# A graph network with nucleus attention on one core: a fifth row buffer, and step 2 turns its rows by VectorE and DRAM

## The chip, the cores and the metric

The kernel runs on one core of a Trainium2 chip. The core has TensorE (PE, with its weight loads shown as PEld), VectorE (DVE), ScalarE (ACT), GpSimd (POOL) and SyncE (SP, which here issues nearly all DMAs). The metric is the device time of one execution in microseconds; lower is better. All data are float32.

## The reference

There are N = 3327 nodes with 256 features. Two layers follow one another, each with a layer norm and a ReLU ahead of it and a residual around it. Layer 0 makes two steps; each multiplies one state by a row-normed copy of the adjacency (R) and another by a top-p attention matrix (A), which is made new in each step.

```python
def _top_p_attention(X, W1, W2, W3):
    logits = (X @ W1.T @ W2.T) @ (X @ W3.T).T
    probs = softmax(logits)
    # keep the largest of each row until they hold 0.9 of its sum
    ...
    return A / A.sum(-1)

R = S + eye; R = R / R.sum(-1)
Z = 0; Xf = X; Xa = X
for n in range(2):
    A = _top_p_attention(Xa, W1, W2, W3)
    Xf = R @ Xf
    Xa = A @ Xa
    Z = Z + Xf @ U1[n].T + Xa @ U2[n].T
h = layernorm(X + Z) * ln_g + ln_b
```

Layer 1 is attention over the neighbours of the adjacency with four heads (leaky ReLU, softmax over neighbours, ELU).

## The kernel before

The 3327 rows are padded to 26 tiles ("rows" below) of 128. The program has three stages. **Step 1** and **step 2** (`n` = 0 and 1) are the two steps of layer 0. The **last stage** is layer 1: four blocks of 832 target nodes, each a loop over 26 source tiles, with masks on ScalarE, exponents on VectorE (L1733) and products on PE (L1749, L1763).

A row of a step goes through this chain:

- `Row.logits` (PE, L898) multiplies the row's queries with all keys into PSUM. The operands are `qq` (queries of all rows) and `kt` (keys), both held twice, on the two halves of the partitions. `exps` (ACT, L913) writes the exponentials into a buffer `e`, 128 x 3328. There are four such buffers.
- A threshold for the top-p cut is searched: `count` (ACT, L950) counts above a threshold, `step` (L952 to L996) makes the next threshold from the count with short instructions on one column. The first two thresholds of a row are stepped on GpSimd; step 2 has a third, stepped on VectorE. Starting values come from `stats` (L809), which gets mean and variance of each row's logits from the keys' moments `gk`.
- `window`, `sort` and `choose` (VectorE, L1006 to L1059) find the exact cut in the values under the threshold. `drop` (VectorE, L1064) zeroes what is cut off, in four parts.
- The row must be turned[...]. `BLOCKED` (L50) says in how many rows of each step this is done by blocks; before the change it is (26, 0). With blocks, `turn_blocks` (VectorE, L1102) turns 32x32 blocks in place, `put_blocks` writes 1024 columns to DRAM (L1106), and four `get_blocks` (L1111) read them back rearranged; `attend_blocks` (PE, L1118) multiplies. Only the last two column tiles go through PE. Without blocks, `turn` (PE, L1077) turns 128x128 pieces by the identity into PSUM, ACT or DVE copies them to `et` (L1088), and `attend` (PE, L1095) multiplies.
- In step 1, `finish1` makes keys and queries of step 2 from the result, and the values `ys` (first half: the next step's right operand, fetched later as `rhs`; second half: the part of Z). In step 2, `finish2` adds up, norms and projects for layer 1.

Beside it, `full` computes R @ Xf for each row: loads of the transposed adjacency (`at`, four buffers), 26 matmuls into `accf` (L1142), and an evacuation: ACT copies `accf` to `f` (L1149) or DVE adds to it straight from PSUM (L1154). `add` then completes it on DVE: in step 1 the division by the row sum (L1169 to L1171, into `c`), in step 2 a multiply and add with a `base` fetched from `ys` (L1173, into `main`). `project_u` has multiplied `main` and `c` by the U1 matrices beforehand, so step 2's full products go straight into Z.

The order of all instructions is found by a planner (`Plan`, L472). Each piece of work is `put` with an engine, a length, a rank, what it needs, and the buffers it takes and gives back; `lag` is the reckoned time from its end until its result can be used. `either` lets the planner choose ACT or DVE. The planner runs these through a clock and writes the queues in that order; on the chip each engine then takes its instructions in that fixed order. Full products have the rank min(1 + 1.15 t, 27) in step 1, and rows the rank of their number (step 2: plus 30), lower first.

Of the kernel before, what the change touches and what calls it, by code (L numbers as in the profile page):

```python
# [15 lines left out]
ALU = mybir.AluOpType  # L16
# [33 lines left out]
BLOCKED = (NT, 0)  # L50
# [537 lines left out]
def fast(  # L588
# [31 lines left out]
    kts = spill.tile([P, NT * P], F32, name="kts")  # L620
    qqs = spill.tile([P, NT, P], F32, name="qqs")
# [26 lines left out]
    with ExitStack() as l0:  # L648
# [17 lines left out]
        qq = wpool.tile([P, NT, P], F32, name="qq")  # L666

# [5 lines left out]
        u2 = wpool.tile([P, 2, 2 * D], F32, name="u2")  # L673
# [3 lines left out]
        gk = wpool.tile([P, 2 * DA + 1], F32, name="gk")  # L677
        GP.memset(gk, 0.0)
        GP.tensor_copy(gk[:DA, DA + 1 :], ident[:DA, :DA])
# [22 lines left out]
        def weights():  # L702
# [10 lines left out]
            for n in range(STEPS):  # L713
                cols = slice((1 - n) * D, (2 - n) * D)
                uloads.append(
                    plan.put(
                        "SP", 0.4, -196.5 + n, nc.sync.dma_start, u1[:, :, cols],
                        u1t[n].rearrange("(c p) o -> p c o", p=P), lag=8.0,
                    )
                )  # L720
                plan.put(
                    "SP", 0.4, -150.0, nc.sync.dma_start, u2[:, :, cols], u2t[n].rearrange("(c p) o -> p c o", p=P)
                )
# [25 lines left out]

        def layer1_loads():  # L750
# [24 lines left out]
        def moments(t, kq, ps_k, ps_g):  # L775
# [4 lines left out]
            held = {}  # L780
# [28 lines left out]
        def stats(lo, hi, rank, needs, scaled):  # L809
# [6 lines left out]
            def product(held, t0, m):  # L816

                held["ps"] = ps_x.tile([P, 3, 2 * DA + 1], F32, name="px")
                for k in range(m):
                    T.matmul(held["ps"][:, k, :], qq[:, t0 + k, :], gk, start=True, stop=True)  # L820
# [6 lines left out]
            def square(held, t0, m):  # L827
                qg = held["qg"]
                for k in range(m):
                    junk = small.tile([P, DA], F32, name="qj", bufs=1)  # L830
                    V.scalar_tensor_tensor(
                        junk, qg[:, k, :DA], 1.0, qg[:, k, DA + 1 :], ALU.mult, ALU.mult,
# [4 lines left out]
            for t0 in range(lo, hi, 3):  # L837
                held, m = {}, min(3, hi - t0)
# [24 lines left out]
            return plan.put("DVE", 0.6, rank, rest, needs=[a])  # L863

        plan = Plan(dict(rows=1, mvs=3, pl=2, px=2, acca=1, accf=1, et=3, at=4, y=1, e2=3, mask=2, **BUFS))

        class Row:
# [10 lines left out]
            def open(self):  # L878
                self.e = epool.tile([P, NP], F32, name="e")
# [6 lines left out]
            def logits(self, k):  # L886
# [7 lines left out]
                for r in range(2):  # L894
# [5 lines left out]
                        qq[half, self.i, :],  # L900
# [51 lines left out]
            def step(self, k, eng):  # L952
# [16 lines left out]
                else:  # L969
                    TS(self.q, t, (self.t0, self.t1)[k - 1], 0.5, ALU.add, ALU.mult)  # L970
                    TS(self.u, s[k], s[k - 1], self.q, ALU.subtract, ALU.mult)
# [8 lines left out]
                else:  # L980
# [5 lines left out]
                TS(self.q, self.g, 0.5, 1.0 / AIM[self.n], ALU.mult, ALU.add)  # L986
                invert(self.q)
# [136 lines left out]
        JC = 4  # L1124

        class Full:
# [24 lines left out]

            def take(self):
                self.f = small.tile([P, H * FH + 2 * H], F32, name="f", bufs=BUFS["f"])
                V.tensor_add(self.f[:, :D], self.acc[:, :D], self.src[:, self.t, :D])  # L1154
                if self.n == 0:
                    V.tensor_copy(self.f[:, D : D + 1], self.acc[:, D:])
# [6 lines left out]
            def add(self):  # L1163
# [4 lines left out]
                if self.n == 0:  # L1168
                    V.tensor_scalar(rs, self.f[:, D : D + 1], 1.0, None, ALU.add)  # L1169
                    V.reciprocal(rs, rs)  # L1170
                    V.scalar_tensor_tensor(here, f, rs, here, ALU.mult, ALU.add)  # L1171
                else:
                    V.scalar_tensor_tensor(main[:, self.t, :D], f, rs, self.base, ALU.mult, ALU.add)  # L1173
# [4 lines left out]
        def keys_summed(t, kq, ps_k, ps_g, rank, needs, tags, give):  # L1178
            turn, copy, product, gather = moments(t, kq, ps_k, ps_g)
# [32 lines left out]
        def prepare(t, measured):  # L1212
# [28 lines left out]
            def keys():  # L1241
                GP.tensor_copy(kt[mine, cols], held["kq"][mine])
                GP.tensor_copy(qq[other, t, :], held["kq"][other])

            def double():
                nc.sync.dma_start(qq[mine, t, :], held["kq"][other])
# [7 lines left out]
            k = plan.put("POOL", 0.7, r, keys, needs=[a])  # L1254
            q = plan.put("SP", 0.2, r, double, needs=[a])
            g = t % 4 == 0 and keys_summed(
                t, lambda: held["kq"], lambda: ps_a.tile([P, P], F32, name="acca"),
# [3 lines left out]
            return [k, q], g  # L1261
# [18 lines left out]
        def finish1(row, done, rank):  # L1280
# [27 lines left out]
            def queries():  # L1308
                GP.tensor_copy(qq[other, t, :], held["kq"][other])

            def spread():
                kq = held["kq"]
                if not direct:
                    nc.sync.dma_start(kts[mine, cols], kq[mine])
                    nc.sync.dma_start(qqs[other, t, :], kq[other])
                nc.sync.dma_start((qq if direct else qqs)[mine, t, :], kq[other])

            def project_u2():
                ps = held["pu"] = ps_x.tile([P, 2 * D], F32, name="px")
                for k in range(2):  # L1320
                    T.matmul(ps, held["xt"][:, k, :], u2[:, k, :], start=(k == 0), stop=(k == 1))
# [5 lines left out]
            def add():  # L1327
                y = held["y"]
                GP.tensor_add(y[:, 1, :], y[:, 1, :], rhs[0][:, t, :])

# [14 lines left out]
            kq = [a]  # L1345
            if direct:
                kq = [
                    plan.put("DVE", 0.2, r, keys, needs=[a, drawn[0]]),
                    plan.put("POOL", 0.4, r, queries, needs=[a, drawn[0]]),
                ]  # L1350
            kq.append(plan.put("SP", 0.3, r, spread, needs=[a, drawn[0] if direct else None]))
            g = t % 4 == 0 and keys_summed(
                t, lambda: held["kq"], lambda: ps_x.tile([P, P], F32, name="px"),
                lambda: ps_x.tile([P, DA + 1], F32, name="px"), r, [a, guessed[0]], ("px", "px"), [],
            ) or None
            plan.put("SP", 0.02, r, lambda: None, needs=[kq, g], give=["kq"], lag=0.0)
            a = plan.put("PE", 1.75, r + 0.1, project_u2, needs=[x_], take=["px"])
            a = plan.put("ACT", 0.56, r + 0.1, stage, needs=[a], take=["ystage"], give=["px", "xt"])
            a = plan.put("POOL", 0.8, r + 0.3, add, needs=[a])
            y = plan.put("SP", 0.1, r + 0.3, store, needs=[a], give=["ystage"], lag=3.0)  # L1360
            return kq, g, y

        def fetch_keys(r):
            half = slice(r * DA, r * DA + DA)
            w = max(half_of(t)[2].stop for t in range(LAST + 1) if side(t) == r)
            nc.sync.dma_start(kt[half, :w], kts[half, :w])

        def fetch_queries(lo, hi):
            nc.sync.dma_start(qq[:, lo:hi, :], qqs[:, lo:hi, :])
# [6 lines left out]
        def finish2(row, done, z, rank):  # L1376
# [64 lines left out]
            x_ = plan.put("SP", 0.1, r - 1.5, fetch, needs=[row.pieces["guess"]], take=["ystage"], lag=3.0)  # L1441
# [4 lines left out]
            s_ = plan.put("SP", 0.1, r, store, needs=[a])  # L1446
# [35 lines left out]
        def search(row, rank, keys, stats_of, fresh):  # L1482
# [4 lines left out]
            for g in range(2):  # L1487

                def logits(g=g):
# [4 lines left out]
                    "PE", 1.95 - 0.67 * g, rank - 2.5, logits, needs=[keys, fresh, a], take=["pl", "pl"] + ["e", "sc"] * (1 - g)  # L1494
# [10 lines left out]
            for j in range(2):  # L1505
# [4 lines left out]
                a = plan.put("POOL", (3.8, 4.7)[j], rank - (2.0, 1.6)[j], row.step, j, GP, needs=[got, more])  # L1510
# [21 lines left out]
        GROUPS = -(-NT // 4)  # L1532

        def attention(row, rank, total, drops, right):
            a = None
            if row.i < BLOCKED[row.n]:
                come = []
                for g in range(3):
                    b = plan.put("DVE", 1.25, rank - 1.001, row.turn_blocks, g, needs=[drops[g]])
                    b = plan.put("SP", 0.5, rank - 1.0, row.put_blocks, g, needs=[b], lag=3.5)  # L1540
                    b = plan.put("POOL", 0.02, -90.0, lambda: None, needs=[b], lag=0.0)
                    come.append(
                        [plan.put("SP", 0.45, rank - 1.0, row.get_blocks, g, o, needs=[b], lag=3.5) for o in range(4)]
# [6 lines left out]
                for j in (0, 4, 8, 12, 24, 16, 20):  # L1550
                    if j == 24:
# [4 lines left out]
                        take=["acca"] * (j == 0), give=["e"] * (j == 20),  # L1556
                    )
                return plan.put("ACT", 0.4, rank - 2.7, row.attended, needs=[a, total], take=["xa"], give=["acca", "sc"])
            for g in range(GROUPS):
# [4 lines left out]
                    give=["e"] * (g == GROUPS - 1),  # L1564
# [518 lines left out]
```

## Time and profile before

| what | us |
|---|---|
| three runs, median (lowest to highest) | 2159.17 (2158.55 to 2160.39) |
| the profiled execution | 2158.39 |
| its span | 2156.6 |
| first and last result of a row, step 1 (L1122) | 132.3 and 828.8 |
| first and last result of a row, step 2 (L1122) | 935.6 and 1674.4 |
| last matmul stage (L1749), main part from | 1676.9 |

The result of a row is its instruction at L1122, the only one per row that scales the attended sum. Between 828.8 and about 914 no row's attention runs: the keys of step 2 depend on all rows of step 1, and PE fills the time with full products. The mean granted TensorE clock is 0.995 of full speed. In the profile, a fp32 matmul appears as two instructions and a transpose as one. Instructions of PE overlap, so the mean ns of one is longer than its share of the queue; starts are the better measure.

### The profile page before, as it was taken

To read this page: it belongs to the slowest core of one execution; us is meant where nothing else is said; L and a number is where in the kernel's file an instruction comes from. 1 tells how busy PE (TensorE), PEld (TensorE's weight loads), DVE (VectorE), ACT (ScalarE), POOL (GpSimd) and SP (SyncE) were. 2 spreads that over 40 slices of the span, in tenths; PEclk is the share of its full clock that TensorE was granted. 3 is DMA by queue.
4 is the path that set the end of the run, shared out by engine and by line. 5 is a ranking of instruction groups with operands and counts; after the bars stand their busy time and mean duration, and the time that the engine had idled before them with its cause. 6 is when DMAs were issued, how large, how long until landed. Compare 5 with 4: busy or idle time off the path is not lost. (4 is left out here: it accounts for less than half of the span.)

```text
span 2156.6 us, 35324 instructions
## 1 busy us (share of the span) xinstructions
PE 2098.1 (97%) x11247; PEld 1464.1 (68%) x11247; DVE 1757.0 (81%) x4436; ACT 1324.9 (61%) x2444; POOL 945.9 (44%) x2259
## 2 busy tenths in 40 slices
PE   8999999999999999999999999999999999999997
PEld 6577777777777777778877888888888433333332
DVE  5579887878777781578999899978878999989895
ACT  4677565665456621687777767777773556565552
POOL 5367555555554630367667666567553100000001
PEclk9999999999999999999999999999999999999999
DMA  4077777777776796522222222222224545354441
GB/s 122 22 172 186 184 181 177 177 177 173 187 173 162 154 240 181 150 62 76 65 64 59 62 62 62 74 76 75 68 70 134 153 128 160 114 153 117 117 124 33
DMA packets 398243, 265.52 MB, mean 123 GB/s; under 512 B 181370, under 2 KB 352096, under 8 KB 398048
## 3 DMA queue, kind: packets, MB, share of 16 engines
q1 hardware_dynamic: 397152, 262.97, 47.1%
q8 instruction: 91, 1.49, 0.3%
q14 instruction: 104, 0.85, 0.1%
q10 hardware_dynamic: 896, 0.21, 0.0%
HBM read 205.31 MB, written 56.84 MB: 122 GB/s over the span
## 5 line engine op out<-in xcount | busy, mean ns | idle before, releaser
L950 ACT ACTIVATE junk<-e,sc 128x3327 fp8e5<-128x3327 f32 x182 | 558.2, 3067 | 65.2 <-POOL sc L995 64.0
L1095 PE MATMUL acca<-rhs,et 128*128 128x256 f32 x1456 | 336.4, 379 | 0.0
L1142 PE MATMUL accf<-main,at 128*128 128x257 f32 x1352 | 314.0, 383 | 8.3 <-DMA at<-in_adjt_dram 6.6
L1142 PE MATMUL accf<-c,at 128*128 128x256 f32 x1352 | 313.4, 382 | 3.5 <-DVE f L1154 2.5
L1118 PE MATMUL acca<-rhs,e 128*128 128x256 f32 x1248 | 284.6, 383 | 22.3 <-DMA e<-blocks 21.5
L1095 PEld LDWEIGHTS acca<-rhs,et 128*128 128x128 f32 x1456 | 268.9, 190 | 32.3
L1142 PEld LDWEIGHTS accf<-main,at 128*128 128x128 f32 x1352 | 252.0, 190 | 57.0 <-issue 10.9
L1142 PEld LDWEIGHTS accf<-c,at 128*128 128x128 f32 x1352 | 249.8, 190 | 49.1 <-issue 9.7
L1118 PEld LDWEIGHTS acca<-rhs,e 128*128 128x128 f32 x1248 | 243.8, 197 | 57.5 <-issue 23.6
L1006 DVE SCALAR_TENSOR_TENSOR y<-e,sc 128x1639 f32<-128x1639 f32 x104 | 208.6, 2006 | 58.2 <-POOL sc L992 55.9
L1011 DVE MAX8 cands<-y 128x8 f32<-128x205 f32 (+1 forms) x832 | 243.0, 362 | 3.6
L913 ACT ACTIVATE e<-pl 128x1024 f32<-128x1024 f32 x208 | 183.7, 889 | 68.4 <-PE pl L898 66.2
L1064 DVE SCALAR_TENSOR_TENSOR e<-e,thr 128x1024 f32<-128x1024 f32 x208 | 219.0, 1075 | 4.8 <-DVE thr L1059 2.8
L1888 POOL TENSOR_TENSOR qq<-qq 128x256 f32<-128x256 f32 x4 | 3.0, 756 | 446.3 <-ACT qq L1884 446.2
L1722 ACT ACTIVATE et<-at 128x448 bf16<-128x448 f32 (+1 forms) x204 | 112.2, 550 | 130.1 <-DVE e L1733 75.1
L1749 PE MATMUL pl<-e,main 128*64 128x416 f32 x1024 | 188.8, 516 | 0.0
L898 PE MATMUL pl<-kt,qq 64*128 64x512 f32 (+1 forms) x832 | 173.6, 535 | 0.0
L1749 PEld LDWEIGHTS pl<-e,main 128*64 128x64 f32 x1024 | 70.0, 137 | 109.4 <-issue 92.3
L1733 DVE SCALAR_TENSOR_TENSOR e<-c,low,et 128x832 f32<-128x832 f32 x128 | 128.9, 1072 | 6.3 <-issue 3.2
L898 PEld LDWEIGHTS pl<-kt,qq 64*128 64x128 f32 x832 | 71.5, 186 | 83.8 <-issue 75.7
L1721 ACT ACTIVATE at<-at 128x448 f32<-128x448 f32 (+1 forms) x204 | 110.5, 542 | 26.2 <-DMA at<-in_adjt_dram 26.2
L1088 ACT COPY et<-px 128x512 f32<-128x512 f32 (+1 forms) x129 | 67.3, 533 | 95.1 <-PE px L1077 47.8
(546 smaller groups left out, 3408.8 us busy)
## 6 DMA issues: line engine op xcount, KB each, us to landing
at<-in_adjt_dram SPq DMA_DIRECT2D x414, 256.0 KB
blocks<-e SPq DMA_DIRECT2D x78, 512.0 KB
e<-blocks SPq DMA_DIRECT2D x312, 128.0 KB
at<-in_adjt_dram SPq DMA_DIRECT2D x102, 192.0 KB
at<-in_adjt_dram SPq DMA_DIRECT2D x52, 128.0 KB
ys<-ystage SPq DMA_DIRECT2D x26, 256.0 KB
rhs<-in_x_dram SPq DMA_DIRECT2D x26, 128.0 KB
ystage<-in_x_dram SPq DMA_DIRECT2D x26, 128.0 KB
```

What stands on the lines that cost most here:

```text
L898: T.matmul(pl[:, lo : lo + m], qq[half, self.i, :], kt[half, 512 * k : 512 * k + m], start=True, stop=True,)
L913: S.activation(to, pl, AF.Exp, accum_out=(self.p0, self.p1, self.p2, self.p3)[k],)
L950: S.activation(junk[:, :N], self.e[:, :N], fn, bias=t, scale=-1.0, accum_out=dst, saturate=False)
L1006: V.scalar_tensor_tensor(self.y[:, : hi - lo], self.e[:, lo:hi], self.up, self.e[:, lo:hi], ALU.is_lt, ALU.mult, accum_out=(self.h0, self. ...
L1011: V.max(self.cands[:, a * PIECES // 2 + k, :], self.y[:, at[k] - lo : at[k + 1] - lo])
L1064: V.scalar_tensor_tensor(piece, piece, self.thr[:, o : o + 1], piece, ALU.is_gt, ALU.mult)
L1095: T.matmul(self.acc, et[:, j - 4 * g, :], rhs[self.n][:, j, :], start=(j == 0), stop=j == NT - 1 and self.i >= BLOCKED[self.n],)
L1118: T.matmul(self.acc, lhs, rhs[self.n][:, j, :], start=(j == 0), stop=stop and j == js[-1])
L1142: T.matmul(self.acc[:, : self.w], self.at[j // JC][:, j % JC, :], self.src[:, j, : self.w], start=(j == 0), stop=(j == NT - 1),)
L1722: S.activation(to, src, AF.Sign)
L1733: V.scalar_tensor_tensor(held["e"][:, k, :], extra["both"][b % 2][:, k, :], low[:, j, k : k + 1], held["mask"], ALU.max, ALU.mult,)
L1749: T.matmul(q["acc"][a][k * FH : (k + 1) * FH, c, :C], main[:, j, h * FH : (h + 1) * FH], held["e"][:, h, c * C : (c + 1) * C], start=(j == 0),
```

## The change

- `BLOCKED` becomes (26, 23): in step 2, too, rows 0 to 22 are turned by VectorE and DRAM; the last three still go through PE.
- There is a fifth buffer for `e`. It takes the room of `qq` (same size), every fifth row uses it (`own_e`), and the last stage, which also uses that room, now waits for those rows. Queries no longer lie in `qq`: they are kept in DRAM (`kqs`, one tile for each step) and fetched in groups of four rows into `qg` (two buffers); rows 0 to 7 of step 1 are put there directly.
- `stats` runs for each group of four rows (seven times a step, before three) and has its own `gk` for each step.
- In step 2 the full product is scaled from PSUM into `main` by ACT or DVE, and `base` is added by GpSimd. The term with `src` that DVE used to add there is now added in `finish1`, on DVE, to what is stored in `ys`; so the store of a row in step 1 needs that row's full product.
- The second of step 2's three thresholds (stepped on GpSimd) takes over slope and divisor of the first and does not compute them anew. The third stays on VectorE.
- The U2 matrices are loaded later, into the room of `late`, and the loads of layer 1 come after the last store of `ys`.
- Lengths and lags given to the planner change: DMA issues on SP 0.4 to 1.3 us for 0.1 to 0.5, the lag of `put_blocks` 6.0 for 3.5, of `get_blocks` 4.5 for 3.5.

```diff
-BLOCKED = (NT, 0)
+BLOCKED = (NT, NT - 3)
...
-        qq = wpool.tile([P, NT, P], F32, name="qq")
...
-        gk = wpool.tile([P, 2 * DA + 1], F32, name="gk")
+        gks = [wpool.tile([P, 2 * DA + 1], F32, name=f"gk{n}") for n in range(STEPS)]
...
+        own_e = [[("e", "e5")[i % 5 == 2 - n] for i in range(NT)] for n in range(STEPS)]
...
             def open(self):
-                self.e = epool.tile([P, NP], F32, name="e")
+                if own_e[self.n][self.i] == "e":
+                    self.e = epool.tile([P, NP], F32, name="e")
+                else:
+                    self.e = wpool.tile([P, NP], F32, name="qq")
...
                 if k == 0:
                     TS(self.g, self.u, cs[:, self.i : self.i + 1], 0.25, ALU.mult, ALU.min)
-                else:
+                elif last:
                     TT(self.w, self.k2, self.g, ALU.mult)
                     TS(self.w, self.u, self.dt, self.w, ALU.mult, ALU.add)
                     TS(self.v, self.u, self.u, self.k2, ALU.mult, ALU.add)
                     invert(self.v)
                     TT(self.g, self.w, self.v, ALU.mult)
-                TS(self.q, self.g, 0.5, 1.0 / AIM[self.n], ALU.mult, ALU.add)
-                invert(self.q)
+                if k == 0 or last:
+                    TS(self.q, self.g, 0.5, 1.0 / AIM[self.n], ALU.mult, ALU.add)
+                    invert(self.q)
...
+            def scaled_by_s(self):
+                S.activation(main[:, self.t, :D], self.acc[:, :D], AF.Copy, scale=rsum[:, self.t : self.t + 1])
+            def scaled_by_v(self):
+                V.tensor_scalar(main[:, self.t, :D], self.acc[:, :D], rsum[:, self.t : self.t + 1], None, ALU.mult)
...
+            def add_base(self):
+                GP.tensor_add(main[:, self.t, :D], main[:, self.t, :D], self.base)
...
+        def fetch_queries(n, g):
+            lo, hi = 4 * g, min(4 * g + 4, NT)
+            to = qg[n, g] = small.tile([P, 4, P], F32, name="qg", bufs=2)
+            for t0, t1 in ((lo, hi),) if g < 6 else ((24, 25), (25, 26)):
+                other = half_of(t0)[1]
+                for r in range(2):
+                    nc.sync.dma_start(to[r * DA : r * DA + DA, t0 - lo : t1 - lo, :], kqs[n][other, t0:t1, :])
...
+            def own():
+                y = held["y"][:, 1, :]
+                V.scalar_tensor_tensor(y, c[:, t, :], rsum[:, t : t + 1], y, ALU.mult, ALU.add)
...
             a = plan.put("POOL", 0.8, r + 0.3, add, needs=[a])
-            y = plan.put("SP", 0.1, r + 0.3, store, needs=[a], give=["ystage"], lag=3.0)
-            return kq, g, y
+            a = plan.put("DVE", 0.43, r + 0.3, own, needs=[a, fulls[t]], hold=0.4)
+            y = plan.put("SP", 0.5, r + 0.3, store, needs=[a], give=["ystage"], lag=3.0)
+            return kq, q, g, y
...
-                    b = plan.put("SP", 0.5, rank - 1.0, row.put_blocks, g, needs=[b], lag=3.5)
+                    b = plan.put("SP", 0.5, rank - 1.0, row.put_blocks, g, needs=[b], lag=6.0)
...
-                        [plan.put("SP", 0.45, rank - 1.0, row.get_blocks, g, o, needs=[b], lag=3.5) for o in range(4)]
+                        [plan.put("SP", 0.6, rank - 1.0, row.get_blocks, g, o, needs=[b], lag=4.5) for o in range(4)]
...
+            if n == 1:
+                a = plan.either(
+                    ("ACT", 0.4, f.scaled_by_s), ("DVE", 0.45, f.scaled_by_v), -90.0, needs=[a], give=["accf"]
+                )
+                b = plan.put("SP", 0.4, rank, f.fetch, needs=[loads[-1], stored[t]], take=["base"], lag=3.0)
+                return plan.put("POOL", 0.8, rank - 1.2, f.add_base, needs=[a, b], give=["base"])
...
-                return plan.put("DVE", 0.88, -90.0, f.add, needs=[a, b], give=["f", "base"], hold=0.85)
...
-                a = plan.put("SP", 0.5, base + 4.0, layer1, needs=[used, done[3]], take=["et"], lag=8.0)
+                a = plan.put("SP", 1.8, base + NT + 1.0, layer1, needs=[used, stored], take=["et"], lag=8.0)
```

## Prediction, made before the changed kernel was seen

> **What bounds the kernel now.** I read the busy shares first, then busy time by stretch, then the costs of the lines concerned, then the waits.
>
> ```profile
> PE 2098.1 (97%) x11247; PEld 1464.1 (68%) x11247; DVE 1757.0 (81%) x4436; ACT 1324.9 (61%) x2444; POOL 945.9 (44%) x2259
> ```
>
> PE has 97%, so it looks like the only engine worth unloading. The stretches below say otherwise. The first is step 1 from row 3 to row 25, the second step 2 from row 4 to row 25 (88 drops, so 22 rows), the third its first 14 rows, the fourth all of step 2 from VectorE's first threshold step to the last drop.
>
> ```profile
> core 0: us, PE busy (x) PEld busy (x) DVE busy (x) ACT busy (x) POOL busy (x), PEclk, DMA share, GB/s
> 312.68:798.39 485.71, 463.25 (x2109) 365.56 (x2108) 375.90 (x969) 278.73 (x470) 265.69 (x644) 0.99 0.76 177
> 1008.88:1653.94 645.06, 639.69 (x3243) 521.81 (x3242) 569.95 (x1781) 467.72 (x770) 399.92 (x933) 1.00 0.25 73
> 1008.88:1404.00 395.12, 390.84 (x1983) 316.30 (x1982) 365.19 (x1136) 295.20 (x482) 251.63 (x595) 1.00 0.22 64
> 889.00:1663.00 774.00, 768.11 (x3893) 624.39 (x3890) 676.26 (x2144) 563.93 (x931) 474.76 (x1104) 1.00 0.26 74
> ```
>
> Step 1 leaves PE idle for 22.5 us of 486 (4.6%) and VectorE for a quarter. In step 2 PE is busy for 99%, but VectorE has 92% in the third stretch, beside a full PE. Two engines are nearly full there; the change takes work from one and gives some to the other.
>
> ```profile
> PE acca L1118 <- DMA e<-blocks: 21.5, 16, 3.1
> DVE keep L1041 <- POOL sc L1015: 4.1, 6, 1.5
> DVE et L1088 <- PE acca L1095: 2.5, 4, 1.5
> ```
>
> The first line (waits of the whole run) is most of step 1's PE idle: blocks that come back from DRAM late. The other two head VectorE's waits in the third stretch, which sum to 8.9 us, 2.3% of it. Its other 21 us of idle are the gaps of some tens of ns between short instructions: VectorE is as full there as such a sequence lets it be.
>
> [...]
>
> **The change part by part.**
>
> ```profile
> L1077 PE MATMUL px<-ident,e 128*128 128x128 f32 x728 | 106.3, 274 | 2.7 <-DVE e L1064 2.1 <-DVE et L1088 0.2
> 920.06 0.60 PE L1077 MATMUL px<-ident,e 128*128 128x128 f32 x4
> 920.50 1.89 PE L1095 MATMUL acca<-rhs,et 128*128 128x256 f32 x8
> L1102 DVE STREAM_TRANSPOSE e<-e 128x1024 f32<-128x1024 f32 x78 | 97.4, 1249 | 2.6
> L1088 DVE COPY et<-px 128x512 f32<-128x512 f32 x57 | 38.5, 682 | 24.3 <-PE acca L1095 12.9 <-PE px L1077 10.7 <-ACT e L913 0.5
> L1154 DVE TENSOR_TENSOR f<-accf,c 128x256 f32<-128x256 f32 x10 | 4.2, 419 | 9.4 <-PE accf L1142 9.4
> L1167 DVE TENSOR_TENSOR f<-f,c 128x256 f32<-128x256 f32 x15 | 6.3, 417 | 9.2 <-ACT f L1149 9.2
> L1173 DVE SCALAR_TENSOR_TENSOR main<-f,rsum,base 128x256 f32<-128x256 f32 x25 | 12.3, 490 | 0.9
> ```
>
> *TensorE, step 2.* 23 rows lose 24 turns each, 552. Four take 0.44 us in the queue (920.06 to 920.50), 0.11 each: -60.7 us. The attending matmuls cost the same (383 against 379 ns). 768.1 becomes about 707, so PE no longer bounds step 2.
>
> *VectorE, step 2* (774 us, busy 676.3). Gone: 23/26 of the 38.5 us of full copies, -34.1; the additions at L1154, L1167, L1173, -22.8. New: 3 x 23 turns of 1.249, +86.2; the scaling of the neighbour product, taken by either engine, if VectorE takes 10 as at L1154, +4.2 (between 0 and +11); seven groups of statistics in place of three, each seven short instructions of 0.17, and those that lay before 889, +7 (5 to 10); the layer-1 scores, which lay hidden in step 1 (4 x 0.424 + 4 x 0.42), now follow the last store, +3.4. Sum 720. The gaps: 774 - 676.3 - 57.6 of named waits = 40.1, 5.9% of busy, so 763 engaged. Waits at the third stretch's 2.3% add 17.5: 780.5, against 774. **Step 2 gets 6.5 us longer**; PE, then some 73 us idle, cannot help. Bounds: no wait at all, -11; all 57.6 us of today's waits, +47.
>
> *GpSimd and ScalarE.* The shorter second threshold drops seven GpSimd steps a row, two of them powers near 0.75 us; the new addition puts about 0.8 back (L1389's shape). ScalarE loses most of its turned copies. Neither is over 73% in step 2: nothing, and if the cover is gone the threshold chain of a row is longer, which the fifth buffer absorbs.
>
> *Fifth buffer, longer lags.* In step 1 the planner now reckons 6.0 and 4.5 us for the trip through DRAM, not 3.5, and rows may run one further ahead. That aims at the 21.5 us of waits; I take three quarters, -16.1, between 0 and -28 (the at loads' 6.6 too). The new addition in finish1 (0.49 us on VectorE) is covered by VectorE's free quarter. But it waits for the row's full product: the ys store behind it on SP, ystage (two buffers) and PSUM wait too. Full products run behind rows by their rank, so this binds only near the end of step 1.
>
> *Transfers.* Step 2 gains 3 puts and 12 gets a row. Its DMA share goes from 0.26 to about step 1's 0.76. On SP 12 gets of some 0.5 us, 3 puts of 0.4 and the at loads make about 11 us of 29. A store of x1s that waits for VectorE has the gets behind it: late blocks cost PE, which has slack now.
>
> *Handover.* Queries come in groups of four ahead of use and the keys by two chained fetches: nothing. The fetch of rhs (839.5 to 881.9 now) must wait for all full products (887), so ends near 932. Row 0's attention, at 914 now, gets its blocks near 926: cover is PE's other full products, and a loss of 6 us if VectorE runs out of buffers. At the end of step 2 PE has no full product left over: -2.6 (the piece of accf at 1674.3).
>
> The sum, against the profiled 2158.4 us (span 2156.6): +6.5 - 16.1 - 2.6 = -12.2, so 2146; the median of the runs is 0.8 higher, so **2147 us**.
>
> **The rivals.**
>
> *A, TensorE keeps the pace.* Step 2 gets PE's gain, less blocks that come late as in step 1 (15.8 us in 17 rows, 0.93 x 23 = 21.4): -60.7 + 21.4 - 16.1 - 2.6 gives 2100. For it: the last stage has stretches where VectorE is 100% busy, and VectorE's late rows were loose (205 of 250 us). Against: 720 us of busy would have to fit 735.
>
> *B, slower: VectorE inherits the bound and keeps its waits.* Its place is VectorE's queue in step 2. A waiting instruction stops the windows, drops and turns of all rows behind it. If the 57.6 us of waits stay, that is 40.1 more than reckoned: 2187. It decides from about 30 us of waits in step 2 (17.5 + 12.2). For it: VectorE now meets DMA-dependent rows, and SP's order. Against: 32.8 of the 57.6 fell after 1404, where PE held VectorE back, and the instructions that waited most (L1154, L1167, L1088) go.
>
> *C, step 1 gains nothing* and the late rhs costs 6 us: 2147 + 16 + 6 = 2169. For it: the store that waits for full products. Against: 1.3 us of PE idle a row is there to be had.
>
> *D, it does not do what it says*: the second threshold reuses the first's slope; should a window miss, the whole slow program runs and the time is at least doubled. Nothing in the profile speaks for it; under 1%, left out of the range.
>
> **How the numbers follow.** Forecast 0.46, A 0.24, B 0.22, C 0.08. The forecast's own range is 2125 to 2165; a measurement here can tell about 0.2%, 4.3 us. Of the forecast's 0.46, 0.31 lies below 2154.9, 0.10 within, 0.05 above. So faster 0.31 + 0.24 = 0.55, same 0.10, slower 0.05 + 0.22 + 0.08 = 0.35. The range, 2102 to 2187, cuts half of A and of B.
>
> **What would show it.** Right: step 2's VectorE at 97% or more with gaps, PE near 90% in the same stretch; from 889 to the last drop 765 to 795 us; the wait for blocks in step 1 at 5 us or less. Wrong: PE still at 99% in step 2 (A); named waits of VectorE over 30 us there (B); step 1's row period still 28.6 us (C).

## The result, and the profile after

The median of four runs is 2128.14 us (2127.11 to 2129.65), against 2159.12 before: a ratio of 0.9856, 95% interval 0.9839 to 0.9873. That is 31 us less; the forecast was 12 less. The profiled execution has a span of 2125.3 us, 31.3 below the 2156.6 of before, and the spans are what is split up below.

The share of busy time of each engine, from the page of the changed kernel:

```profile
PE 2049.7 (96%) x10695; PEld 1415.8 (67%) x10695; DVE 1797.6 (85%) x4491; ACT 1290.6 (61%) x2380; POOL 927.4 (44%) x2092
```

PE lost 48 us of work, VectorE gained 41, and PE still shows 96%. Where the time went needs marks that both traces have. I take the end of the last full product of step 1 on PE (it comes last of PE's work for step 1), the first reciprocal of a third threshold on VectorE, the end of the last drop of step 2, and the end of the span:

| us | before | after | difference |
|---|---|---|---|
| last full product of step 1 ends | 887.6 | 856.1 | -31.5 |
| from there to the first third threshold | 4.8 | 3.6 | -1.2 |
| from there to the last drop (step 2's length) | 768.9 | 770.6 | +1.7 |
| from there to the end | 495.3 | 495.0 | -0.3 |

Step 2, in which nearly all of the edits lie, gained nothing. The whole gain lies in step 1. Busy time by stretch shows what it is made of: first before, from 90 us to the end of the last full product of step 1 (length of the stretch, then busy time and number of instructions of each engine):

```profile
core 0: us, PE busy (x) PEld busy (x) DVE busy (x) ACT busy (x) POOL busy (x), PEclk, DMA share, GB/s
90.00:887.60 797.60, 765.96 (x3503) 603.68 (x3502) 589.59 (x1584) 450.10 (x771) 412.72 (x995) 1.00 0.75 178
```

The same view after; its first line is step 2, from the first third threshold to the last drop, its second is step 1:

```profile
core 0: us, PE busy (x) PEld busy (x) DVE busy (x) ACT busy (x) POOL busy (x), PEclk, DMA share, GB/s
858.00:1630.00 772.00, 726.62 (x3350) 580.95 (x3349) 707.72 (x2141) 531.59 (x867) 448.42 (x959) 0.98 0.75 179
90.00:856.00 766.00, 756.57 (x3490) 601.82 (x3489) 596.55 (x1645) 447.92 (x768) 425.05 (x989) 1.00 0.79 181
```

In step 1 PE's idle time, length less busy, falls from 31.6 to 9.4 us: -22.2. Its busy time falls too, by 9.4, for 13 recorded instructions fewer out of 3503. Eleven of the 13 are products with U1 (L1272; L1299 after) which the changed kernel has done before 90 us; they make 5.0 of the 9.4. Counted from the start of the program, nothing crosses the first mark; before, then after:

```profile
0.00:887.60 887.60, 846.88 (x3862) 654.83 (x3863) 632.15 (x1751) 499.42 (x890) 456.07 (x1138) 0.99 0.70 168
0.00:856.10 856.10, 839.80 (x3860) 652.17 (x3860) 639.84 (x1807) 499.73 (x898) 462.90 (x1116) 1.00 0.72 168
```

Idle time is 24.4 us less, and busy time 7.1 less for two instructions fewer. Of the 7.1, at most 3.4 are the granted clock (an estimate, half of the time by which its stretches at half speed are shorter: 13.6 us before, 6.8 after); the products that read blocks (L1118; L1126 after) are busy for 280.7 us where it was 284.6. What makes the rest is open. PE's waits from 90 us up to the same point after, the two longest in sum:

```profile
PE accf L1151 <- DMA at<-in_adjt_dram: 6.1, 2, 4.4
PE px L1085 <- DVE e L1072: 1.1, 2, 1.0
```

The 21.5 us of waits for blocks that headed this list are gone altogether; the loads of the transposed adjacency cost about what they did (6.6 before).

In step 2 the queue of VectorE has these waits from 858 to 1630, and no others over 0.15 us (us in total, times, longest):

```profile
DVE main L1165 <- PE accf L1151: 9.1, 4, 8.0
DVE sd L1453 <- ACT f L1447: 3.6, 3, 1.7
DVE et L1096 <- PE px L1085: 2.9, 4, 1.0
DVE xt L1438 <- PE px L1434: 2.6, 3, 1.5
DVE sc L978 <- ACT junk L957: 2.5, 1, 2.5
DVE xa L1412 <- ACT xa L1130: 2.4, 1, 2.4
```

They sum to 23.1. Busy 707.7 and 23.1 leave 41.2 us of gaps between instructions, 5.8% of busy. VectorE is full by the measure that the prediction used, and PE has 94%.

### The profile page after: what moved, and what is told of

Same layout as the page of the kernel before. It is cut to its first block, busy times and chain, and to the rows that moved or that the text cites. A ratio compares the mean times of both kernels' runs of the same rounds, so it can differ in the third digit from the quotient of the medians.

```text
span 2125.3 us, 34576 instructions
## 1 busy us (share of the span) xinstructions
PE 2049.7 (96%) x10695; PEld 1415.8 (67%) x10695; DVE 1797.6 (85%) x4491; ACT 1290.6 (61%) x2380; POOL 927.4 (44%) x2092
## 5 line engine op out<-in xcount | busy, mean ns | idle before, releaser
L957 ACT ACTIVATE junk<-e,sc 128x3327 fp8e5<-128x3327 f32 x147 | 450.7, 3066 | 60.4 <-POOL sc L1003 58.9
L1126 PE MATMUL acca<-rhs,e 128*128 128x256 f32 x1872 | 425.0, 381 | 9.4 <-DMA e<-blocks 8.9
L1126 PEld LDWEIGHTS acca<-rhs,e 128*128 128x128 f32 x1872 | 365.2, 197 | 53.8 <-issue 14.1
L1151 PEld LDWEIGHTS accf<-c,at 128*128 128x128 f32 x1352 | 252.1, 191 | 73.5 <-issue 13.6
L920 ACT ACTIVATE e<-pl 128x1024 f32<-128x1024 f32 (+1 forms) x168 | 152.3, 918 | 55.6 <-PE pl L905 52.4
L1014 DVE SCALAR_TENSOR_TENSOR y<-e,sc 128x1639 f32<-128x1639 f32 x84 | 163.9, 1952 | 24.7 <-POOL sc L1000 23.9
L1072 DVE SCALAR_TENSOR_TENSOR e<-e,thr 128x1024 f32<-128x1024 f32 (+1 forms) x168 | 178.8, 1068 | 3.2 <-DMA at<-in_adjt_dram 0.5
L905 PE MATMUL pl<-kt,qg 64*128 64x512 f32 (+1 forms) x832 | 173.5, 535 | 1.5 <-ACT e L920 1.5
L1110 DVE STREAM_TRANSPOSE e<-e 128x1024 f32<-128x1024 f32 x117 | 146.0, 1248 | 3.8
L905 PEld LDWEIGHTS pl<-kt,qg 64*128 64x128 f32 x832 | 71.6, 186 | 84.7 <-issue 74.7
L1754 DVE SCALAR_TENSOR_TENSOR e<-qq,low,et 128x832 f32<-128x832 f32 x120 | 120.7, 1078 | 5.7 <-ACT at L1742 3.8
L957 ACT ACTIVATE junk<-qq,sc 128x3327 fp8e5<-128x3327 f32 x35 | 107.2, 3064 | 12.8 <-POOL sc L1003 12.6
```

Source lines behind the costliest of these rows:

```text
L905: T.matmul(pl[:, lo : lo + m], qg[self.n, self.i // 4][half, self.i % 4, :], kt[half, 512 * k : 512 * k + m], start=True, stop=True,)
L920: S.activation(to, pl, AF.Exp, accum_out=(self.p0, self.p1, self.p2, self.p3)[k],)
L957: S.activation(junk[:, :N], self.e[:, :N], fn, bias=t, scale=-1.0, accum_out=dst, saturate=False)
L1014: V.scalar_tensor_tensor(self.y[:, : hi - lo], self.e[:, lo:hi], self.up, self.e[:, lo:hi], ALU.is_lt, ALU.mult, accum_out=(self.h0, self. ...
L1072: V.scalar_tensor_tensor(piece, piece, self.thr[:, o : o + 1], piece, ALU.is_gt, ALU.mult)
L1110: V.transpose(part, part)
```

## The experiments

### Which edit gave step 1 its 31 us: lags or buffer

Theory L: step 1 gained because the planner reckons the trip through DRAM as long as it is. Rival: the fifth buffer gained it. The kernel before gets four numbers of the change and nothing else (the expectations take the two of a read as one); the changed kernel gets the four old ones; and the changed kernel loses its fifth buffer.

```diff
# before_lags (after_old_lags is the same, backwards, in the changed kernel)
- row.put_blocks, g, needs=[b], lag=3.5)
+ row.put_blocks, g, needs=[b], lag=6.0)
- plan.put("SP", 0.45, rank - 1.0, row.get_blocks, g, o, needs=[b], lag=3.5)
+ plan.put("SP", 0.6, rank - 1.0, row.get_blocks, g, o, needs=[b], lag=4.5)
- plan.put("SP", 0.1, rank, f.load, q, ...)
+ plan.put("SP", 0.4, rank, f.load, q, ...)
# before_put_get: the first two alone
# after_four_e
- own_e = [[("e", "e5")[i % 5 == 2 - n] for i in range(NT)] for n in range(STEPS)]
+ own_e = [["e" for i in range(NT)] for n in range(STEPS)]
```

> The kernel before with three numbers given to the planner changed and nothing else: lag of put_blocks 6.0 for 3.5, get_blocks length 0.6 and lag 4.5 for 0.45 and 3.5, length of the at loads 0.4 for 0.1. Theory L (the honest lags end TensorE's waits for blocks in step 1, and that is the gain): waits of PE for blocks fall from 21.5 us to under 5, the first third-threshold step moves from 889 to about 862, time 2133 (2126 to 2142). Theory E (the fifth buffer is what lets rows run ahead): block waits stay above 12 us, time 2150 or more. Theory T (the gain comes from the turns taken off TensorE in step 2): 2155 to 2163.

> The kernel before with the lags of 6.0 and 4.5 and the length of 0.6 for a read of blocks, but the old length of 0.1 for the loads of the transposed adjacency. If the lags do it: 2136 to 2145, as with all three numbers (2139.8). If SP's queue does it, where the plan thought 7 loads a row to cost 0.7 us and they cost some 2.8: 2150 to 2160, most of the 18 us gone.

> The changed kernel with those three numbers as before (3.5 and 3.5, 0.45, 0.1). Theory L: PE waits for blocks come back in step 1 and now in step 2 too, time 2150 or more. Theory E: step 1 stays free of waits, time 2124 to 2136. Theory T: 2124 to 2140.

> The changed kernel with four buffers for e in both steps. Theory L: step 1 keeps its gain (first third-threshold step within 5 us of 858), and step 2, whose rows hold e some 20 us longer with blocks, gets longer: 2135 to 2165. Theory E: the first third-threshold step falls back to 880 or later, time 2155 or more. Theory T: 2128 to 2140.

| kernel | median us | ratio to before, 95% | last full product of step 1 | step 2's length |
|---|---|---|---|---|
| before_lags | 2139.84 | 0.9910 (0.9894 to 0.9927) | 869.9 | 768.1 |
| before_put_get | 2137.06 | 0.9898 (0.9882 to 0.9914) | 867.9 | 767.9 |
| after_old_lags | 2197.53 | 1.0169 (1.0148 to 1.0190) | 890.3 | 807.8 |
| after_four_e | 2147.00 | 0.9940 (0.9922 to 0.9958) | 869.2 | 779.9 |

The lags alone, in the kernel before, bring 18 to 20 us of step 1, and the length of the loads on SP shows no part in it. "Lags" stands for three numbers: 6.0, 4.5, and 0.6 for the issue of a read; which of them does it was not tried one by one. PE's waits for blocks fall to 7.0 us, and to 6.0 in before_put_get, not under the 5 that I had expected. In before_lags:

```profile
PE acca L1118 <- DMA e<-blocks: 7.0, 5, 1.8
```

Without the lags, the fifth buffer and all other edits bring nothing in step 1 (890.3 against 887.6) and make the program slower: in step 2 rows now use blocks too, and PE waits for them. PE's waits in step 2 of after_old_lags:

```profile
PE px L1085 <- DVE e L1072: 15.7, 4, 9.4
PE acca L1126 <- DMA e<-blocks: 15.1, 12, 4.0
PE px L822 <- DMA qg<-kqs: 9.8, 1, 9.8
PE acca L1126 <- DMA qq<-blocks: 6.2, 6, 1.9
```

Against 9.3 us for blocks in step 2 after (`e` and `qq` together), that is 12.0 more. That the other waits follow from these is my reading and not shown.

What the trip looks like in the queue of SP, at the first row of the kernel before (start, length, line, tiles, number):

```profile
103.93 0.38 SPq L1106 DMA_DIRECT2D blocks<-e  x1
...
106.38 0.38 SPq L1106 DMA_DIRECT2D blocks<-e  x1
...
108.84 0.38 SPq L1106 DMA_DIRECT2D blocks<-e  x1
109.31 0.46 SPq L1136 DMA_DIRECT2D at<-in_adjt_dram  x1
109.86 9.75 SPq L1111 DMA_DIRECT2D e<-blocks  x12
```

The 12 reads need 9.75 us to be issued, 0.8 each, where the plan had 0.45. The first read starts 5.9 us after the first write, but two more writes and three loads stand between them in the queue, so this is no measure of the write alone: in the next row a read starts 3.2 us after its write (142.41 and 139.19), which the plan's 3.5 covers. When a block lands is not in the trace; that it came late shows in PE's waits. Order and time then part. PE's instructions start in the trace of the kernel before in the order in which the program issues them, in all of their 1189 stretches of one line and one output; so one that was put at a place where the plan has its data stands there and waits, with PE's other work behind it: 16 times for blocks, 21.5 us in all, 3.1 at the longest.

after_four_e fell where theory L had the whole, but not where it had step 1 (first third threshold at 872.8, not within 5 us of 858): taken alone, it says that a fifth buffer gives 13 us there. I took this for settled, and it was not.

### The luck of one order

A still longer lag ought to have cost nothing or, with the buffers short, a little.

```diff
- row.put_blocks, ... lag=6.0)      row.get_blocks, ... lag=4.5)
+ row.put_blocks, ... lag=8.0)      row.get_blocks, ... lag=6.0)   # after_long_lags
```

> The changed kernel with 8.0 and 6.0 us reckoned for the two halves of the trip through DRAM in place of 6.0 and 4.5. Theory L (the lags gain what they cover of real lateness): TensorE's waits for blocks in step 1 are at nothing already, so step 1's last full product stays within 3 us of 856 and the whole within 5 us of 2128. Rival T (a longer lag holds e longer by the plan, 3.5 us a row): five buffers run short, step 1 or step 2 longer by 5 to 20 us: 2133 to 2150.

Measured: 2132.73 (0.9885, 0.9866 to 0.9904), step 1's last product at 867.2, step 2's length 764.5. Neither theory has that: 11 us lost in step 1 and 6 gained in step 2. So two more lags, each with five and with four buffers:

> The changed kernel with lags of 5.0 and 4.0 us (put, get) in place of 6.0 and 4.5. Theory L (what counts is the trip's real lateness; 3.5 and 3.5 lie under it, 6.0 and 4.5 over it): between the two, nearer to the long ones: step 1's last full product 855 to 868, the whole 2128 to 2145. Rival Z (each planned order is a draw, some 10 us up or down whatever the lag): step 1 anywhere from 850 to 880.

> The changed kernel with lags of 7.0 and 5.2 us. Theory L: between 6.0/4.5 (856.1) and 8.0/6.0 (867.2): step 1's last full product 855 to 867, the whole 2126 to 2134. Rival Z as in the run before.

> The changed kernel with four row buffers only, and lags of 5.0 and 4.0 us. If the fifth buffer is worth some 13 us in step 1 at any lag that covers the trip: last full product 867 to 880, at least 8 us behind the same lags with five buffers; the whole 2143 to 2165. If the 13 us at 6.0 and 4.5 was the luck of one planned order (Z): within 5 us of five buffers, on either side.

> The same four buffers, lags of 7.0 and 5.2 us. Fifth buffer real: last full product 868 to 882, at least 8 us behind the same lags with five, and the longer hold costs more with four than with five; the whole 2145 to 2170. Luck of the order: within 5 us of five buffers.

And two nudges, which change a lag by a tenth of a microsecond and with it the planned order (some 1200 lines of difference for each, when the lists of PE's instructions in the traces are compared with that of the changed kernel), but nothing that it stands for:

```diff
- row.put_blocks, ... lag=6.0)
+ row.put_blocks, ... lag=6.1)      # after_nudge_1
- row.get_blocks, ... lag=4.5)
+ row.get_blocks, ... lag=4.4)      # after_nudge_2
```

> The changed kernel with a put lag of 6.1 us in place of 6.0, nothing else. A tenth of a microsecond can't cover or miss anything real, yet the planned order differs in hundreds of places. Theory Z (part of the gain is the luck of one order): step 1's last full product is some 5 to 12 us later than 856, near 865, the mean of the three lags that cover the trip, and the whole is 2133 to 2148. Rival F (the 13 us belong to the fifth buffer): within 3 us of 856.1, the whole 2125 to 2133.

> The same with a get lag of 4.4 us in place of 4.5. Z and F as in the run before; the two together also give the spread of the step's length: Z expects the two at least 4 us apart in the whole.

| put / get lag | five: median (ratio, 95%) | five: step 1's end, step 2's length | four: median (ratio, 95%) | four: step 1's end, step 2's length |
|---|---|---|---|---|
| 5.0 / 4.0 | 2162.18 (1.0016, 1.0009 to 1.0024) | 863.8, 790.9 | 2169.52 (1.0050, 1.0033 to 1.0067) | 880.4, 791.5 |
| 6.0 / 4.5 | 2128.14 (0.9856, 0.9839 to 0.9873) | 856.1, 770.6 | 2147.00 (0.9940, 0.9922 to 0.9958) | 869.2, 779.9 |
| 6.1 / 4.5 | 2148.35 (0.9943, 0.9927 to 0.9960) | 873.9, 773.6 | - | - |
| 6.0 / 4.4 | 2136.59 (0.9889, 0.9872 to 0.9905) | 857.6, 778.5 | - | - |
| 7.0 / 5.2 | 2144.99 (0.9935, 0.9913 to 0.9957) | 871.8, 776.8 | 2144.10 (0.9941, 0.9919 to 0.9964) | 864.5, 780.2 |
| 8.0 / 6.0 | 2132.73 (0.9885, 0.9866 to 0.9904) | 867.2, 764.5 | - | - |

Of the expectations, few held. The pair at 5.0 and 4.0 speaks for the buffer in step 1, but the whole is far over the 2145 I gave as its end; the pair at 7.0 and 5.2 has five buffers behind four. The first nudge is slower than even theory Z had it; in the second step 1 stays, as F says, and step 2 gets longer, as F doesn't. A tenth of a microsecond costs 20 us in one nudge and 8 in the other. PE's waits in step 1 of the first nudge, up to its last full product:

```profile
PE px L1085 <- ACT ystage L1345: 7.3, 4, 3.8
PE px L1317 <- ACT xa L1130: 5.8, 6, 2.5
PE accf L1151 <- DVE rest L1038: 3.8, 1, 3.8
PE px L1341 <- DVE gk L806: 1.4, 1, 1.4
PE acca L1126 <- DMA e<-blocks: 1.4, 2, 0.9
```

Of these only the last is for blocks from DRAM. The others are pieces of PE's work that this order placed just too early behind ScalarE or VectorE; the changed kernel's own order happens to have only 2.1 us of the kind. The five orders whose lags lie near or over 6.0 and 4.5 have a mean of 2138.2 us, 21 below before, with step 1's end at 865.3 on average (856 to 874) and step 2's length at 772.8 (764 to 779). Of the 31 us, then, about 21 belong to the change and 10 to the order that it drew, the best of the five, as far as the one order of the kernel before can stand for it. The old kernel with nothing but the new lags (2139.84 and 2137.06) lies at this mean. So beyond the lags, the fifth buffer, the turns by VectorE and DRAM in step 2 and the other edits together show no gain.

The fifth buffer: three pairs give -16.6, -13.1 and +7.3 us in step 1. With lags that cover the trip the two kernels of four buffers (mean 866.9) lie where the five of five do (865.3). So a gain of step 1 by the buffer is not shown; the first expectation for after_four_e, within 5 us, would have held for an average order. In step 2 both pairs with covering lags favour five (-9.3 and -3.4), and 779.9 and 780.2 lie above all five: some 7 us, at the edge of the spread. With 5.0 and 4.0 step 2 is 18 us over the mean of five buffers and 11 over that of four: there the lag seems to decide, not the buffer.

### Who holds step 2

In step 2 nothing was gained although PE had 41 us less to do. First, the exchange by itself, undone:

```diff
- BLOCKED = (NT, NT - 3)
+ BLOCKED = (NT, 0)                 # after_step2_pe
```

> The changed kernel with all rows of step 2 turned by TensorE again, all else kept. Theories L and E (step 2's exchange of TensorE for VectorE time is worth nothing): 2128, between 2116 and 2140, with PE at 98% or more in step 2 and VectorE under 92%. Theory T: 2155 or more.

2132.71 us (0.9877, 0.9861 to 0.9894): the exchange is worth 4.6 us, less than one order differs from the next. PE has 758.7 of 767 us there, 99%, and VectorE 672.6; after, PE 726.6 of 772 and VectorE 707.7. One bound was given for another at the same height.

Then each side is loaded. The last four MAX8 of a row of step 2 are issued twice (26 x 4 x 0.36 = 37.5 us of VectorE alone, told to the planner), in both kernels:

```diff
- for k in range(part * PIECES // 4, (part + 1) * PIECES // 4):
+ for k in [*range(part * PIECES // 4, (part + 1) * PIECES // 4)] * (2 if (self.n, a, part) == (1, 1, 1) else 1):
```

> The changed kernel with the last four MAX8 of each row of step 2 issued a second time (same result, 4 x 0.36 = 1.44 us of VectorE a row, 37.5 in all, known to the planner). Theory V: nearly all of it shows, 2128 + 30 to 42 = 2158 to 2170. Theory P: at most 10 of it shows, 2128 to 2138.

> The same padding in the kernel before, where VectorE has 98 us of idle in step 2, 58 of them in waits. Theory V: half of it or less shows, 2159 to 2178, and less than in the changed kernel. If both kernels lengthen alike, VectorE bound both.

after_pad took 2162.51 (1.0024, 1.0016 to 1.0033), 34 us over the changed kernel, step 2's length 811.1; before_pad 2163.89 (1.0034, 1.0022 to 1.0045), 6 us over its own, 775.8. Before, some 31 of the 37.5 us hide under PE; after, 34 of them show. The 34 are more than the 20 us between the best and the worst of the five orders; the 6 are not.

Last, the third threshold of step 2, some 3.35 us of VectorE a row by the plan, goes to GpSimd in both kernels:

```diff
- a = plan.put("DVE", 3.35, rank - 1.3, row.step, 2, V, needs=[a])
+ a = plan.put("POOL", 4.7, rank - 1.3, row.step, 2, GP, needs=[a])    # after_third_pool, before_third_pool
# after_third_half: ("POOL", 6.8) and GP for even rows, ("DVE", 3.35) and V for odd ones
+ a = plan.either(("POOL", 6.8, lambda: row.step(2, GP)), ("DVE", 3.35, lambda: row.step(2, V)), rank - 1.3, needs=[a])   # after_third_either
```

> The changed kernel with the third threshold of step 2 stepped on GpSimd (length 4.7 for the planner). It takes about 3.3 us a row off VectorE, 86 of its 708 us, and puts 4.7 on GpSimd. Theory V (VectorE sets step 2's pace): step 2 shortens until TensorE binds at its 727 us of busy, so by 25 to 40 us: 2090 to 2105, with PE at 98% and VectorE under 88% in step 2. Theory P (late blocks and evacuations that TensorE waits for set the pace, VectorE only fills the time): 2120 to 2136. Theory G (the longer chain through GpSimd decides): above 2136.

> The same edit in the kernel before. There TensorE is at 99% in step 2, so by theory V (whose other half is that TensorE binds there) nothing is to be had: 2150 to 2163. If VectorE had been the bound already, 2140 or less.

> The changed kernel, with the third threshold of step 2 on GpSimd for the 13 even rows only, and 6.8 us given to the planner for it there (the step took 5.4 to 8.6 us when all rows had it, not the 4.7 given). Theory V (VectorE holds step 2): 13 rows save some 3.3 us of VectorE each, 43 us less its waits; as all 26 rows gained 18 us with 38 us of VectorE waiting for GpSimd, half of the rows should wait for less than a third of that: 2098 to 2112, at or below the version with all rows (2109.7). Rival G (any GpSimd step in the chain delays its row's window and VectorE queues behind it): 2112 to 2128.

> The same, but for each row the planner takes whichever of GpSimd (6.8 us) or VectorE (3.35 us) comes first. Theory V: the planner leaves most of the steps on VectorE, where the step is half as long, so the gain is at most that of every second row: 2100 to 2125. Rival G as there: not below 2120.

| kernel | median us | ratio to before, 95% | last drop of step 2 |
|---|---|---|---|
| after_third_pool | 2109.73 | 0.9773 (0.9752 to 0.9794) | 1624.3 |
| before_third_pool | 2177.98 | 1.0098 (1.0078 to 1.0119) | 1679.2 |
| after_third_half | 2108.29 | 0.9766 (0.9750 to 0.9783) | 1609.7 |
| after_third_either | 2099.24 | 0.9734 (0.9717 to 0.9750) | 1599.8 |

The same edit gains 18 us where VectorE holds step 2 and loses 20 where PE does. The gain is less than theory V had it (2090 to 2105, with PE at 98%; PE has 727.1 of 766 us, 95%). The loss was not expected at all: VectorE's windows wait 36.6 us for the longer chain on GpSimd there, VectorE waits 47.7 us for PE at L1418 (0.7 before), and PE 9.0 us for dropped rows (1.8 before). In after_third_pool that chain has the largest share of VectorE's waits and so, as I read it, keeps the gain small; the two longest in its step 2:

```profile
DVE y L1014 <- POOL sc L1000: 43.7, 14, 9.3
DVE et L1096 <- PE px L1085: 25.5, 11, 9.8
```

The step on GpSimd took 5.7 to 10.4 us there, 7 in the middle (the expectations' 5.4 to 8.6 is too narrow), where I had given the planner 4.7. With 6.8, and the choice left to the planner, GpSimd takes 17 rows and VectorE 9 (18 reciprocals of two a row are left on it). I had expected most to stay on VectorE, and a time of 2100 or more. Waits (the four longest) and stretch of after_third_either in step 2:

```profile
DVE y L1014 <- POOL sc L1000: 14.0, 6, 3.5
DVE main L1165 <- PE accf L1151: 9.3, 4, 7.0
DVE sd L1453 <- ACT f L1447: 7.0, 3, 6.1
DVE et L1096 <- PE px L1085: 5.0, 7, 1.4
```

```profile
858.00:1600.00 742.00, 711.09 (x3316) 575.22 (x3315) 662.46 (x1893) 521.23 (x847) 546.71 (x1213) 0.99 0.78 182
```

PE has 96% and VectorE 89% of a stretch 30 us shorter. Step 1 ends at 855.7 to 857.1 in these three, as in the changed kernel, so they keep its good order there; the gain lies in step 2 alone. after_third_either beats both kernels: 29 us under the changed one, below all five of its orders. Its own order is a single draw too, but 29 us is more than their spread.

## Why the prediction was right or wrong

**Sign, and who bounds what: right.** Step 2 would pass from PE to VectorE and gain nothing; the gain would be step 1's. Padding and the third threshold show it from both sides. *A* (PE keeps the pace) is out, since step 2 did not get shorter; *B* too, as VectorE's waits are 23.1 us, not 30 or more; *C* too: the store that waits for full products did not hold step 1 up, and its fetch of rhs did not stop VectorE in step 2. The first result of a row there comes at 932.6, which is 76.5 us after the end of step 1 where it was 48.0, but VectorE's waits in these first 80 us are 11.5 us, as they were before.

**Step 2, +6.5 forecast, +1.7 measured.** The parts: VectorE busy 707.7 for 720, gaps 41.2 us for 43, waits 23.1 for 17.5 (read in a stretch of 772 us, where the one that matches the forecast's 774 is 775.7). The turns came out as priced (69 x 1.248 = 86.1 for 86.2), the scaling too (8 x 0.48 = 3.9 for 4.2). By its mean over five orders the term was +3.9.

**PE in step 2: forecast 707, measured 726.6.** The count of turns was right, but the clock was 0.98 of full speed there, not 1.00. An estimate from its stretches at half speed, 23.9 us in all from 858 to 1630: at most half of them, 12 of the 20 us. Another 12 instructions of full products fall into the stretch (1352 for 1340 before), some 3 us by 0.23 each. The rest is open. PE was idle for 45 us of the 772, so, as I read it, this cost nothing.

**The step that failed: fifth buffer and longer lags in step 1, "three quarters, -16.1, between 0 and -28".** Measured: -31.5, outside the bounds that I set. Three things were sized wrongly in it. (1) I counted a share of the waits for blocks; all 21.5 us went, and PE's idle time fell by 24.4 from the start of the program. (2) I counted waits alone. PE's busy time fell too, by 7.1 us for the same work, and nothing in the sum stood for it. (3) I took a planned order for a smooth function of its numbers. In the mean of the five orders step 1 ends 22.3 us earlier than before, within my bounds; this one order lies 9.2 beyond that. PE's idle time from 90 us on is 15.9 us in that mean, 15.7 under before. That this is so near the forecast's 16.1 is luck: waits for blocks are 1.9 us or less in all five, and other waits, which the forecast did not have, took their place. The range of the whole held the result; the size did not, and the spread of orders, from 2128 to 2148, was nowhere among its cases. The mechanism was right as to the lags; as to the fifth buffer in step 1 it is not shown.

**Handover, -2.6: -0.3 at the end of step 2, -1.2 at its start.** Near, and small.

**A reading.** The first stretch of the forecast has 68 drops, so it holds rows 8 to 24 of step 1, not 3 to 25. The sums drawn from it use 17 rows and are right.

**What stays open.** The order of the kernel before is one draw too, and its luck was not measured; the two versions of it with new lags (869.9 and 867.9) agree to 2 us. Which of the three numbers of the trip brings the gain is not known. That the shorter threshold on GpSimd and the later loads cost or bring nothing was not tried one by one.

## What to carry to other kernels

Where a program writes the order of all queues from reckoned lengths, a time that is reckoned shorter than it really is can be a bound of its own: here three numbers for the trip through DRAM gave the old kernel 19 to 22 us, while moving some 40 us of work off TensorE showed 4.6, less than one order differs from the next. Work moved between two engines that are both nearly full gained nothing here until a third took a part of it, so look at once for what can leave the new bound: here the planner's free choice between GpSimd and VectorE, with a length nearer the step's real one, gave 29 us more. And before a few per thousand are put down to an edit, nudge a number that means nothing and see how far the time moves.

## What the runs showed that was not expected

In these traces PE's busy time in step 1 goes up with its idle time, and by the estimate below most of that is its clock. In ten versions of the changed kernel, each with 3490 to 3495 instructions of PE recorded from 90 us to the end of step 1, idle and busy time are 9.4 and 756.6 us (after), 11.4 and 756.2 (after_nudge_2), 17.0 and 756.8 (after_lags_5), 17.1 and 757.4 (four_e_lags_7), 17.1 and 760.1 (after_long_lags), 17.7 and 761.5 (after_four_e), 19.8 and 762.0 (after_lags_7), 21.6 and 762.3 (after_nudge_1), 26.2 and 764.2 (four_e_lags_5), 36.0 and 764.3 (after_old_lags). The granted clock reads 1.00 in the first four and 0.99 in the others.

Behind these means the clock has two values only, 1.00 and 0.50, and up to the last drop of step 2 it is 0.50 in stretches of 3.4 us or a multiple of it (3.41 and 6.83 us in the kernel before and in the changed one). Half of their length, an estimate of the most that they can cost, is 1.7 to 3.4 us in the first four versions and 5.1 to 8.5 in the others. Less that, busy time lies between 753 and 757 us in all ten, and little is left to explain. In step 2 the mean is 1.00 where PE is 99% busy (after_step2_pe), 0.98 at 94% (after), 0.97 at 91% (after_old_lags) and 0.95 at 91% with VectorE padded (after_pad).

In the kernel before and in the changed one each of the seven stretches at 0.50 between 90 us and the last drop of step 2 lies behind a gap of 2.0 us or more in PE's work. One case in step 2 of the changed kernel, the last 3.4 us of PE's gap from 903.7 to 908.9 that are still at full clock, then the stretch at 0.50:

```profile
904.70:908.10 3.40, 0.00 (x0) 0.00 (x0) 3.02 (x18) 3.07 (x3) 2.75 (x11) 1.00 1.08 275
908.10:914.90 6.80, 5.96 (x14) 4.80 (x15) 1.64 (x11) 6.64 (x13) 3.96 (x14) 0.50 0.46 147
```

In all twenty traces, from 90 us to the last drop of step 2, PE has 59 gaps of more than 3.4 us that begin at full clock. Each has such a stretch behind it, which begins during the gap or at most 1.4 us after it; the changed kernel has three of them (4.4, 5.2 and 6.0 us), the kernel before none. So have some of the shorter ones: 34 of the 51 between 2.0 and 3.4 us have a stretch that begins during them or within 4.5 us after (4 of 5 in the kernel before and the changed one together), and 7 of the 66 between 1.5 and 2.0 (none of 7 in these two). That the gap brings the stretch on is my reading. By it a wait of 2 us or more could cost a nearly full TensorE more than its own length: an estimate of up to 1.7 us, half of it, for each 3.4 us at half speed.
